# Graph-attention layers on one core: rows of scores asked for one head ahead, and stores of pieces moved to another queue

## The chip, the cores and the metric

The kernel runs on one core of a Trainium2 chip. The metric is the device time of one execution in microseconds, the median of the runs shown. One further execution was taken with the hardware profiler; the times inside the kernel are from it. Engines are called TensorE (PE), VectorE (DVE), ScalarE (ACT), GpSimd (POOL) and SyncE (SP). SyncE here only issues DMAs. A DMA can be issued from SyncE's, ScalarE's or GpSimd's queue; each queue works in order.

## What is computed

Four layers on 3327 nodes with 512 features, a dense 0/1 adjacency of 3327 x 3327. Each layer is x + L(relu(layernorm(x))). Layers 0, 1 and 2 are graph attention with 8, 4 and 8 heads, layer 3 is a mean over neighbours. Cut to what matters:

```python
def gat(h, adj, W, a1, a2):                      # layers 0 to 2, per head
    Wh = h @ W                                   # [N, 512 / heads]
    e = leaky_relu(s1[:, None] + s2[None, :], 0.2)   # s1 = Wh @ a1, s2 = Wh @ a2
    p = softmax(where(adj > 0, e, -inf), axis=-1)    # layer 1 also has self loops
    return elu(p @ Wh)
def mean_layer(h, adj):                          # layer 3
    agg = (adj > 0) @ h / max(deg, 1)
    return relu(concat(h @ Ws + bs, agg @ Wn + bn) @ Wc + bc)
```

## The kernel before

The N x N softmax is never formed. Since leaky_relu is the larger of two lines, exp(s1 + s2) and exp(0.2 (s1 + s2)) both factor into a row term and a column term, and which of the two holds for a pair of nodes is a comparison s1 > -s2. So a head is a product of 0/1 matrices (mask and comparison) with weighted features, done on TensorE, and a row factor afterwards.

**Tiles.** The 3327 nodes are 26 tiles of 128. Rows of the result go in seven *chunks* (six of four tiles, the last of two; `chunks`). The inner index goes in five *groups* of 6, 6, 6, 4 and 4 tiles (`JG`). `attention` loops over chunks, heads and groups.

**A head.** For each head of each chunk:

- the row of scores s1 of the chunk's nodes is loaded, repeated over the 128 partitions, into `s1b` (`score_rows`, L686). `s1b` has two buffers;
- the *node terms* of the head, the weighted features cut into pieces that TensorE can multiply exactly, are loaded group by group into `ab` (L718 in layer 1, ten loads a head; L724 in layers 0 and 2, five loads a head; in layer 0 some are called `abx`). `ab` has six or seven buffers;
- `matrices` compares s1 with each inner tile's s2 on ScalarE (L674) or VectorE (L671) and masks the outcome on VectorE (L678, L680) into `tht` and `gt`. In layer 1 some groups are then cast by `real` (L643) into `ts` or `tv`;
- TensorE multiplies them with `ab` into `acc` (L766, L769 in layer 1, L773 and L776 in the others), in *passes* of two row tiles over all inner tiles. VectorE reduces `acc` (L787, L791) and scales the outcome into `A`.

**Work between the passes.** After each pass `hooks.run` does one step of the work for the next layer. For a finished row tile: `finish` adds the attention's output to x (L873 to L876, stored by L877 from GpSimd), then layer norm (L347 to L354, the small steps L352 to L354 on GpSimd), relu (L359 on ScalarE), the transpose on TensorE (L138, copied out by L142), the projection (L415), the weighting (L446 to L454), and `parts`, which cuts the node terms into a tile `pt`. In layer 2's terms and the first group of layer 1's, `pieces` does it: GpSimd clears `pt` (L381), ScalarE (L393, L399) and GpSimd (L397) fill it. In the other groups of layer 1's terms ScalarE and VectorE fill two tiles `pt` (L470, L473). One step later `send` stores what `parts` put into `L.to_store` (L551), and the scores of a whole chunk (`send_s1`, L522). `pt` has two buffers there.

**Order.** A scheduler of the framework orders the instructions of each engine, by the order of the program and by when it thinks that they are ready; the order on a queue is fixed when the program is built. At a layer's end the last chunk's tiles are taken through the same steps at once, the next layer's combined weights are multiplied (`Fusion`, L183 to L208), and the next layer begins with the first chunk. A tile that is loaded or filled waits until the buffer's last use is over. For layer 0's first head the row is asked for in advance already (`early["s1"]`).

Of the kernel before, what the change touches and what calls it, by code (L numbers as in the profile page):

```python
# [52 lines left out]
def tile_gnn(ctx: ExitStack, tc: tile.TileContext, x, adj, W0, a01, W1, al, ar, W2, a2,  # L53
             Ws, bs, Wn, bn, Wc, bc, out):
    nc = tc.nc
# [9 lines left out]
    chunks = [(t, min(PER, NT - t)) for t in range(0, NT, PER)]  # L65
# [39 lines left out]
    def dims(l):  # L105


        H = heads[l]
        DA = D // H + 1
        AO = -(-(3 * DA + 1) // 8) * 8 if l != 1 else 3 * DA + 1  # L110
        return H, DA, AO, 2 * AO

    abd = []
    for l in range(3):
        H, DA, AO, HW = dims(l)
# [19 lines left out]
    def transposed(src, pool, name, bufs=2, behind=None):  # L135
        tp = ps.tile([P, KC, P], F32, name="tp", bufs=2)
        for k in range(KC):
            tr = nc.tensor.transpose(tp[:, k, :], src[:, k * P:(k + 1) * P], ident)  # L138
            if k == 0 and behind:
                after(tr, behind)  # L140
        dst = pool.tile([P, KC, P], F32, name=name, bufs=bufs)
        copied.append(nc.scalar.copy(dst, tp).ins.name)  # L142
        return dst
# [201 lines left out]
    def norm(xt, pool, behind=None):  # L345
        st = pre.tile([P, 6], F32, name="st", bufs=4)
        bn = nc.vector.bn_stats(st, xt)  # L347
        if behind:
            after(bn, behind)
        mv = pre.tile([P, 4], F32, name="mv", bufs=4)  # L350
        stats.append(nc.vector.bn_aggr(mv[:, 0:2], st).ins.name)
        nc.gpsimd.tensor_scalar(mv[:, 2:3], mv[:, 1:2], EPS, None, op0=ALU.add)  # L352
        nc.gpsimd.tensor_tensor(mv[:, 2:3], mv[:, 2:3], neghalf, ALU.pow)
        nc.gpsimd.tensor_scalar(mv[:, 3:4], mv[:, 0:1], mv[:, 2:3], -1.0, op0=ALU.mult, op1=ALU.mult)  # L354
        return mv

    def normed(xt, mv, pool, behind=None):
        h = pool.tile([P, D], F32, name="h", bufs=2)
        act = nc.scalar.activation(h, xt, AF.Relu, bias=mv[:, 3:4], scale=mv[:, 2:3])  # L359
        if behind:  # L360
            after(act, behind)
        relus.append(act.ins.name)
        return h
# [95 lines left out]
    def parts(L, t, AB, pool, first, behind=None):  # L459

        l = L.l
        g, jj = jwhere[t]
        H, DA, AO, HW = dims(l)
        H2 = H // 2
        if l == 1 and KIND[g] != "b":
            for f in range(2):
                hs = slice(f * H2, (f + 1) * H2)
                pt = pool.tile([P, H2, 2, 2, DA], F32R, name="pt", bufs=2)
                v = pt.rearrange("p h a s d -> p s a h d")
                cp = nc.scalar.copy(v[:, 0], AB[:, :, hs])  # L470
                if behind:
                    after(cp, behind)
                nc.vector.tensor_sub(v[:, 1], AB[:, :, hs], v[:, 0].bitcast(F32))  # L473
                L.to_store.append((abd[l][g][hs, :, :, jj, :].rearrange("h a p w -> p h a w"),
                                   pt.rearrange("p h a s d -> p h a (s d)").bitcast(F32)))
        else:
            pieces(L, t, AB, pool, first, behind)
        if t == JG[g][0] + JG[g][1] - 1:
            js = slice(JG[g][0], t + 1)
            nc.vector.tensor_scalar(L.ks2[:, js], L.s12[:, 1, js, :], BIG, None, op0=ALU.mult)  # L480
            nc.vector.tensor_scalar(L.ns2[:, js], L.s12[:, 1, js, :], -1.0, None, op0=ALU.mult)

    def project_last(L, t, hT, i, behind=None):

        n = pn(t)
        c, kk = where[t]
        g, jj = jwhere[t]
        pw = ps.tile([P, D], F32, name="mm")
        for k in range(KC):
            mm = nc.tensor.matmul(pw, hT[:, k, :], L.w[i][:, k, :], start=(k == 0), stop=(k == KC - 1))  # L490
            if k == 0 and behind:
                after(mm, behind)
        L.mm = mm.ins.name
        if i == 0:
            def add():
                y = pre.tile([P, D], F32, name="AB", bufs=1)
                sm = nc.vector.tensor_add(y, pw, bias)
                if behind:
                    after(sm, stats[-chunks[-1][1]])
                move(nc.sync, y1d[c][kk * P:kk * P + n, :], y, n)  # L500
            if behind:
                return add
            add()
        else:

            pt = pre.tile([P, 2, D], F32R, name="pt")
            nc.scalar.copy(pt[:, 0], pw)
            nc.vector.tensor_sub(pt[:, 1], pw, pt[:, 0].bitcast(F32))
            nc.sync.dma_start(y2d[g][:, jj], pt.bitcast(F32))

    def send_s1(L, t, pool, first):

        c, k = where[t]
        t0, nt = chunks[c]
        if k + 1 < nt:
            return
        H = heads[L.l]
        tps = ps.tile([PER * H, P], F32, name="mm" if first else "tp", bufs=2)
        nc.tensor.transpose(tps[:nt * H], L.s12[:, 0, t0:t0 + nt, :].rearrange("p t h -> p (t h)"), ident)
        s1t = pool.tile([PER * 8, P], F32, name="s1t", bufs=2)  # L520
        nc.scalar.copy(s1t[:nt * H], tps[:nt * H])
        (nc.sync if first else nc.gpsimd).dma_start(s1d[L.l][c].rearrange("h t p -> t h p"), s1t[:nt * H])  # L522

    def node_stages(L, t, get_x, pool, first=False):

        q = {}
        late = L.l == 3 and t >= NT - 4

        def behind():
            return gone[-1] if gone else None  # L530

        def statistics():
            q["mv"] = norm(q["x"], pool, relus[-2] if first and t > 1 else behind())

        def relu():

            q["h"] = normed(q["x"], q["mv"], pool, copied[-1] if t == NT - 1 and not first else behind())

        def turn():
            b = L.mm if t == NT - 1 and not first else behind()  # L540
            q["hT"] = transposed(q["h"], mp, "A", A_BUFS[2], b) if late else transposed(q["h"], pool, "hT", 2, b)

        def own():
            if late:
                left.append(lambda: project_last(L, t, q["hT"], 0, gone[-1]))
            else:
                project_last(L, t, q["hT"], 0)

        def send():
            for to, pt in L.to_store:  # L550
                nc.sync.dma_start(to, pt)  # L551
            L.to_store = []
            send_s1(L, t, pool, first)

        if first:
            stages = [lambda: (q.update(x=get_x()), statistics(), relu(), get_x(7 if t else 2)), turn,
                      lambda: parts(L, t, scaled(L, t, projected(L, t, q["hT"], first, q.get("pws")), pool, first), pool,
                                    first), send]
            if t == 0:
                stages.insert(2, lambda: q.update(pws=projected(L, t, q["hT"], first)))  # L560
            elif t == 1:
                stages[1] = lambda: (turn(), q.update(pws=projected(L, t, q["hT"], first)))
            return stages
        stages = [lambda: q.update(x=get_x()), statistics, relu, turn]
        if L.l == 3:
            return stages + [lambda: project_last(L, t, q["hT"], 1), own]
        return stages + [lambda: q.update(pw=projected(L, t, q["hT"], first)),
                         lambda: q.update(AB=scaled(L, t, q["pw"], pool, first, behind())),
                         lambda: parts(L, t, q["AB"], pool, first, behind()), send]
# [77 lines left out]
    early = {}  # L647
# [35 lines left out]
    def score_rows(l, t0, nt, h):  # L683
        s1b = rp.tile([P, WMAX], F32, name="s1b", bufs=2)
        v = s1b[:, :nt * P].rearrange("p (k i) -> p k i", k=nt)
        nc.sync.dma_start(v, s1d[l][where[t0][0]][h].partition_broadcast(P))  # L686
        return v

    def attention(L, hooks, open_next, close):

        l = L.l
        H, DA, AO, HW = dims(l)
        DK = DA - 1
        masks = mask_tiles(0, l == 1) if l else masks0
        for c, (t0, nt) in enumerate(chunks):
            last = c + 1 == len(chunks)
            A = [mp.tile([P, D], F32, name="A", bufs=A_BUFS[l]) for _ in range(nt)]
            hook = 0
            for h in range(H):
                if last and h == H - 1:  # L700
# [3 lines left out]
                    if fusion:  # L704
                        fusion.load_biases()
                        fusion.load(0, gone[-1])
                        fusion.load(1, gone[-1])
                s1v = early.pop("s1") if "s1" in early else score_rows(l, t0, nt, h)
                ab = []
                for a in range(2 if l == 1 else 1):  # L710
                    row = []
# [19 lines left out]
                for g in range(len(JG)):  # L731
                    if g in early:
                        pv, gv = early.pop(g)
                    else:

                        pt = mp.tile([P, PER * JM * P], FP8, name="tht", bufs=10 if l == 1 else 7)
# [755 lines left out]
```

## Time and profile before

| | |
|---|---|
| median of 3 runs | 3511.09 us (3506.52 to 3512.33) |
| the profiled execution | 3507.08 us, its span 3504.9 us |
| TensorE, VectorE, ScalarE, GpSimd busy | 98%, 75%, 71%, 18% of the span |
| layer 0's attention | from about 180 to 1193 us |
| layer 1's attention | to 2042 us |
| layer 2's attention | to 3158 us, then layer 3 |
| DMA engines | 228 GB/s on average, 65% of their time on SyncE's queue, 7% on GpSimd's |
| rows of scores (L686) | 140 loads, median 6.3 us from issue to landing for 256 KB |
| stores of pieces (L551) | 78, median 5.4 us from issue to landing |

How to read it: the profile's busy time of an engine leaves out waiting and issuing. A "wait" names the instruction that waited and the one that ended its wait. In a timeline a line is a run of like instructions: start, length, engine, source line, operation, what it writes and reads, how many, and in brackets the idle time before and what ended it. L12 is line 12 of the kernel. The clock is the share of full speed that TensorE was granted.

### The profile page before, as it was taken

What the parts mean: (1) busy time and instruction counts of PE and PEld (TensorE: products, weight loads), DVE (VectorE), ACT (ScalarE), POOL (GpSimd) and SP (SyncE); (2) the same over time, 40 slices, a digit from 0 to 9 for tenths busy, and PEclk for the clock granted to TensorE, in tenths of its full rate; (3) what the DMA queues carried; (4) which work ended last, traced back from release to release, by engine and by line L of the source; (5) the groups of instructions that cost most, each with busy time, mean ns of one, the idle gap of its engine ahead of it and who ended that gap; (6) DMA issues with size and microseconds to landing.
All of it is one profiled execution on the core that took longest, in us unless ns stands there. A gap on an engine that the chain in (4) does not pass through costs nothing. (4 is left out here: it accounts for less than half of the span.)

```text
span 3504.9 us, 77607 instructions
## 1 busy us (share of the span) xinstructions
PE 3425.6 (98%) x30751; PEld 3101.0 (88%) x30751; DVE 2634.1 (75%) x5227; ACT 2502.6 (71%) x4113; POOL 620.5 (18%) x858
## 2 busy tenths in 40 slices
PE   7899999999999999999999989999999999999998
PEld 6699999999999788888888879989898989886887
DVE  7788898888888799889888868867776768682221
ACT  5787888878788888888898677767666767572111
POOL 6611222112011202222323320000000001020000
PEclk9999999999999999999999999999999999999999
DMA  7699999999967787877787976655555555586331
GB/s 209 213 287 257 253 262 253 268 259 266 246 200 248 265 289 271 288 261 273 271 287 255 341 265 194 194 179 184 189 161 190 178 176 189 164 295 260 102 109 54
DMA packets 398118, 797.71 MB, mean 228 GB/s; under 512 B 112969, under 2 KB 221844, under 8 KB 397104
## 3 DMA queue, kind: packets, MB, share of 16 engines
q1 hardware_dynamic: 363890, 723.14, 64.7%
q0 software_dynamic: 28128, 62.42, 7.3%
q10 hardware_dynamic: 5726, 7.08, 0.6%
q8 instruction: 245, 4.01, 0.5%
q14 instruction: 129, 1.06, 0.1%
HBM read 663.59 MB, written 129.64 MB: 226 GB/s over the span
## 5 line engine op out<-in xcount | busy, mean ns | idle before, releaser
L674 ACT ACTIVATE gt<-s1b,ks 128x512 fp8e4<-128x512 f32 (+1 forms) x2448 | 1448.1, 677 | 373.8 <-PE acc L776 263.7
L773 PE MATMUL acc<-ab,tht 128*128 128x195 bf16 (+1 forms) x9112 | 1550.3, 248 | 5.4 <-DVE tht L678 4.6
L776 PE MATMUL acc<-ab,gt 128*128 128x195 bf16 (+1 forms) x9112 | 1549.6, 248 | 1.7 <-DVE gt L680 1.4
L776 PEld LDWEIGHTS <-gt 128*128 128x128 fp8e4 x10744 | 1051.2, 98 | 27.1 <-issue 18.6
L773 PEld LDWEIGHTS <-tht 128*128 128x128 fp8e4 x10744 | 1051.4, 98 | 22.0 <-DVE tht L678 9.3
L678 DVE TENSOR_TENSOR tht<-gt,m 128x768 uint32<-128x768 uint32 (+3 forms) x557 | 448.5, 805 | 99.6 <-ACT gt L674 98.0
L680 DVE TENSOR_TENSOR gt<-tht,m 128x768 uint32<-128x768 uint32 (+3 forms) x557 | 447.3, 803 | 9.4
L643 ACT CAST ts<-tht 128x1536 fp32r<-128x1536 fp8e4 x208 | 301.9, 1472 | 95.0 <-PE acc L766 90.0
L671 DVE TENSOR_SCALAR gt<-s1b,ns 128x512 fp8e4<-128x512 f32 (+1 forms) x446 | 223.8, 505 | 161.9 <-PE acc L776 158.4
L766 PE MATMUL acc<-ab,ts 128*128 128x258 f32 x2496 | 333.8, 290 | 5.1 <-ACT ts L643 3.4
L766 PEld LDWEIGHTS acc<-ab,ts 128*128 128x128 f32 x2496 | 313.4, 190 | 13.3 <-ACT ts L643 3.8
L674 ACT ACTIVATE tht<-s1b,ks 128x512 fp8e4<-128x512 f32 (+1 forms) x504 | 308.1, 680 | 3.9 <-DMA s1b<-s 3.2
L1028 PE MATMUL acc<-y,mf 128*128 128x512 f32 x1352 | 309.8, 391 | 0.5 <-DVE mf L1023 0.5
L876 POOL TENSOR_TENSOR xt<-xt,e 128x512 f32<-128x512 f32 x72 | 118.5, 1646 | 1055.7 <-DVE e L875 994.8
L1028 PEld LDWEIGHTS acc<-y,mf 128*128 128x128 f32 x1352 | 253.6, 188 | 56.6 <-DVE mf L1023 0.9
L776 PE MATMUL acc<-abx,gt 128*128 128x195 bf16 (+1 forms) x1632 | 284.5, 248 | 4.2 <-DVE rc L813 2.0
L773 PE MATMUL acc<-abx,tht 128*128 128x195 bf16 (+1 forms) x1632 | 284.6, 248 | 3.7 <-DMA tr<-at 2.2
L791 DVE TENSOR_REDUCE R<-acc 128x130 f32<-128x390 f32 x416 | 214.4, 554 | 88.7 <-PE acc L776 87.7
L1025 ACT CAST mf<-m 128x768 fp32r<-128x768 fp8e4 (+1 forms) x78 | 59.1, 762 | 244.0 <-PE acc L1028 232.2
L769 PE MATMUL acc<-ab,tht 128*128 128x387 bf16 x1248 | 224.0, 328 | 6.7 <-DMA ab<-ab 4.0
L766 PE MATMUL acc<-ab,tv 128*128 128x258 f32 x1664 | 217.3, 283 | 0.0
L766 PEld LDWEIGHTS acc<-ab,tv 128*128 128x128 f32 x1664 | 206.8, 189 | 0.3
(163 smaller groups left out, 3705.4 us busy)
## 6 DMA issues: line engine op xcount, KB each, us to landing
ab<-ab SPq DMA_DIRECT2D x333, 600.0 KB, 5.4
ab<-ab SPq DMA_DIRECT2D x112, 774.0 KB, 6.4
ab<-ab SPq DMA_DIRECT2D x112, 516.0 KB, 5.4
ab<-ab SPq DMA_DIRECT2D x112, 400.0 KB, 3.7
abx<-ab SPq DMA_DIRECT2D x110, 400.0 KB, 7.3
ab<-ab SPq DMA_DIRECT2D x56, 582.0 KB, 7.1
s1b<-s SPq DMA_DIRECT2D x120, 256.0 KB, 6.3
m<-mask SPq DMA_DIRECT2D x69, 384.0 KB, 4.7
```

The lines of the kernel that those rows point to most:

```text
L643: (nc.scalar.copy if KIND[g] == "s" else nc.vector.tensor_copy)(t[:, :k1 - k0, :nj], th[a][g][:, k0:k1])
L671: nc.vector.tensor_scalar(gv[:, :, jj, :], s1v, L.ns2[:, j, h:h + 1], 2.0, op0=ALU.is_gt, op1=ALU.mult, saturate=False)
L674: nc.scalar.activation(gv[:, :, jj, :], s1v, AF.Relu, bias=L.ks2[:, j, h:h + 1], scale=BIG, saturate=False)
L678: nc.vector.tensor_tensor(pu, gu, mu, ALU.bitwise_and)
L680: nc.vector.tensor_tensor(gu, pu, mu, ALU.bitwise_xor)
L766: mm = nc.tensor.matmul(acc[k][:, :2 * DA], thr[g][:, k - ks[0], jj, :], ab[a][g][:, jj, :], start=(j == 0), stop=(j == NT - 1), skip_grou ...
L769: mm = nc.tensor.matmul(acc[k][:, :3 * DA], th[a][g][:, k, jj, :], ab[a][g][:, jj, :3 * DA], start=(j == 0), stop=(j == NT - 1), skip_grou ...
L773: nc.tensor.matmul(acc[k][:, :3 * DA + o], th[0][g][:, k, jj, :], ab[0][g][:, jj, :3 * DA + o], start=(j == 0), stop=False, skip_group_che ...
L776: mm = nc.tensor.matmul(acc[k][:, AO:AO + 3 * DA + o], th[1][g][:, k, jj, :], ab[0][g][:, jj, AO:AO + 3 * DA + o], start=False, stop=(j == ...
L791: nc.vector.tensor_reduce(R[:, k], v.rearrange("p a (s d) -> p a d s", s=3), AX.X, ALU.add)
L876: nc.gpsimd.tensor_add(xt, xt, e)
L1028: nc.tensor.matmul(acc[k], mf[:, jj, :], y2[g][:, jj, s, :], start=(j0 + jj == 0 and s == 0), stop=(j0 + jj == NT - 1 and s == 1))
```

## The change

The row of scores for the next head is asked for in the program just before the present head's `ab` loads: the next head of the same chunk, or the first of the next chunk, or the first head of the next layer. Layer 2's last head asks for none. And `send` issues the stores of pieces from GpSimd's queue.

```diff
         def send():
             for to, pt in L.to_store:
-                nc.sync.dma_start(to, pt)
+                nc.gpsimd.dma_start(to, pt)
             L.to_store = []
             send_s1(L, t, pool, first)
...
                 s1v = early.pop("s1") if "s1" in early else score_rows(l, t0, nt, h)
+                if h + 1 < H:
+                    early["s1"] = score_rows(l, t0, nt, h + 1)
+                elif not last:
+                    early["s1"] = score_rows(l, *chunks[c + 1], 0)
+                elif l < 2:
+                    early["s1"] = score_rows(l + 1, *chunks[0], 0)
                 ab = []
```

The first layer's own terms are not stored by `send` but in `pieces` (L407, L408), which stays on SyncE. The prediction says first, second and third layer for layers 0, 1 and 2.

## The prediction

> **What bounds the kernel now.** I read the head of the page first, then the waits of TensorE stage by stage, the timelines of SyncE's queue and of ScalarE at the stage where TensorE waits, and the windows there.
>
> ```profile
> span 3504.9 us, 77607 instructions
> PE 3425.6 (98%) x30751; PEld 3101.0 (88%) x30751; DVE 2634.1 (75%) x5227; ACT 2502.6 (71%) x4113; POOL 620.5 (18%) x858
> ```
>
> TensorE is the bound: 3425.6 of 3504.9 us busy. All that an edit of queues can win is in the other 79.3 us, and only where a row of scores, an `ab` load or a stored piece is what TensorE waits for. Before 180 us (the first projection) neither part of the change acts, since its stores keep SyncE's queue. From 180 to 1955 us, its waits add up to 18.0 us, of which 2.4 are for an `ab` load and none for a row; after 2110 us nothing waits for scores or pieces. What is left is the turn from the second to the third layer. TensorE's waits in 1955 to 2110 us (in total, times, longest):
>
> ```profile
> PE acc L766 <- ACT ts L643: 3.4, 1, 3.4
> PE acc L773 <- DVE tht L678: 3.4, 1, 3.4
> PE acc L766 <- DMA ab<-ab: 1.7, 1, 1.7
> PE acc L769 <- DMA ab<-ab: 1.6, 1, 1.6
> ...
> PE acc L769 <- DVE tht L678: 0.6, 1, 0.6
> ```
>
> The first and the last of these are the last head of the second layer, which waits for its compares (L674) and their casts (L643). Why the compares are late stands in SyncE's queue, 2003 to 2026 us (start, length, issues), and in ScalarE's timeline:
>
> ```profile
> 2002.80 2.19 SPq L718 DMA_DIRECT2D ab<-ab  x2
> 2005.09 7.60 SPq L551 DMA_DIRECT2D ab<-pt  x2
> 2012.74 0.58 SPq L686 DMA_DIRECT2D s1b<-s  x1
> 2013.41 11.65 SPq L718 DMA_DIRECT2D ab<-ab  x8
> ...
> 2019.41 7.29 ACT L674 ACTIVATE tht<-s1b,ks 128x256 fp8e4<-128x256 f32 x18 [2.26 <-DMA s1b<-s]
> ```
>
> Both things that the change touches are in these lines: the row of scores is asked for at 2012.74, behind two stores of pieces of which the second waits 6.2 us for its copy (L399). The row's buffer had been free since 1972.3, where ScalarE's and VectorE's compares of two heads earlier end. The compares of this head start as the row lands, 2019.41. In the windows the clock shows what such a gap costs besides (columns: PE, PEld, DVE, ACT, POOL busy; clock; DMA):
>
> ```profile
> 2010.00:2015.00 5.00, 5.00 (x38) 4.10 (x37) 3.98 (x6) 2.48 (x7) 3.83 (x6) 1.00 0.70 207
> 2025.00:2030.00 5.00, 1.89 (x10) 1.89 (x11) 5.00 (x15) 4.59 (x8) 0.12 (x1) 0.85 1.03 411
> 2030.00:2035.00 5.00, 5.00 (x35) 4.78 (x35) 3.69 (x8) 4.22 (x6) 0.53 (x1) 0.81 1.02 411
> 2060.00:2065.00 5.00, 2.53 (x9) 1.89 (x10) 3.72 (x5) 5.00 (x12) 0.01 (x1) 0.76 0.18 52
> 2065.00:2070.00 5.00, 4.90 (x29) 3.92 (x28) 4.00 (x7) 3.34 (x9) 2.22 (x3) 0.90 0.27 91
> ```
>
> After each 3.4 us gap the granted clock falls: 0.15 x 5 + 0.19 x 5 = 1.7 us of work lost at the first, 0.24 x 5 + 0.10 x 5 = 1.7 us at the second.
>
> **Part 1, rows one head ahead.** No instruction is added; 140 row requests (L686) move up in program order. In most heads nothing can move in time: there are two `s1b` buffers, so the row of a head waits for the compares of two heads before in either program. The timelines show requests already there: in the first layer, chunk 3, the compares of head 2 end at 673.5 and the row of head 4 goes out at 676.5; in the second layer 1418.8 (last head of chunk 1) and 1419.1 (second head of chunk 2). The queue is not in program order, and requests were already pulled up. So this part is worth nothing, except where SyncE came late: the last head of the second layer (40 us after its buffer was free) and the first of the third (2041.69, where the buffer was free at 1985.7).
>
> Stall A, the last head of the second layer: 0.6 + 3.4 us of wait and 1.7 us of clock, 5.7 us. With the row landed by about 1980 the compares follow the freed mask tiles, and ScalarE is idle enough (2.48 of 5 us in 2010 to 2015). I take all of it.
>
> Stall B, the first head of the third layer: 3.4 + 1.7 = 5.1 us. Here an early row is not all: the compares stand behind the last tile's normalization (L359, 2057.03) in ScalarE's queue and start at 2057.75, although the row asked for at 2041.69 needs only the median 6.3 us to land. The nearest row is the turn from the first to the second layer, where the row was early (asked for at 1172.9) and the compares still began at 1207.32, right behind L359. There TensorE waits 2.1 us for L678, and the clock loses 1.7 us (0.77 and 0.89 in 1210 to 1220): 3.8 us. So B should shrink to that, by 1.3 us; its ends are 0 and 5.1.
>
> What new wait could part 1 make? A request now stands ahead of its predecessor's `ab` loads, and if the queue kept that order these loads would wait for compares. In the third layer, chunk 3, the request for head 5 would stand ahead of the loads of head 4 and wait for the compares of head 3, which end at 2613.5; these loads start at 2628.0 anyway, held by TensorE's use of the buffers. Cover: 14.5 us. In the first layer, chunk 3, it is 673.5 against 670.1 for the loads of head 3, whose matmuls begin at 695.3; a delay of 3.4 us would still leave 18 us. Nothing.
>
> **Part 2, stores from GpSimd's queue.** 78 issues (L551) leave SyncE: 52 of 512 runs each and 26 of 1024. On SyncE each took 0.37 us and the waits before them 126.5 us for copies:
>
> ```profile
> SPq L551 <- ACT pt L399: 88.3, 22, 20.2
> SPq L551 <- DVE pt L473: 38.2, 23, 9.4
> ```
>
> For those on GpSimd, the nearest rows are its own issues: 0.64 us for 128 runs (L877), 0.80 for 512 (L199), from which I estimate 1.1 us for 1024. The sum is 52 x 0.80 + 26 x 1.1 = 70 us, on an engine that is 18% busy; nothing of it is TensorE's. Landing is 4.5 us from GpSimd (L877) against 5.4 from SyncE (L551). Queued behind a store there are the additions (L876), the statistics (L352 to L354), which ScalarE's L359 and then TensorE's transposes need, the clearing of `pt` (L381), and the row stores (L877, L522). But a store's own GpSimd half (L397) stands ahead of it in this queue, and it ends with or after ScalarE's half: 2002.54 against 2001.5, 2012.29 against 2011.7. So the long waits of SyncE mostly vanish rather than move, and the rest has a whole hook step, at least 8.8 us (one pass of 104 matmuls at 84 ns), before TensorE needs it. I take 0 for that.
>
> The gain is on SyncE: the loads of 2013.41 could go at about 2005, when the stores no longer hold them. That is the other half of stall A, not a second gain. For the `ab` waits of 1.6 and 1.7 us at 1975 and 1979, SyncE gets rid of one issue of 0.39 us at 1965.46: 0.4 us.
>
> One rule speaks against the move: the Trainium skill, SBUF — State Buffer, "SBUF: two separate sides", says that GpSimd can't write descriptors while VectorE runs a mode that takes the shared port, and gives 620 ns growing to 3100 ns. The trace's 255 issues from GpSimd took 0.52 to 1.11 us beside a VectorE that is 75% busy, so it doesn't show such a stall; by the page, 78 x 2.5 = 195 us would be an estimate of the delay, still on GpSimd.
>
> **Sum.** 5.7 + 1.3 + 0.4 = 7.4 us. The profiled execution took 3507.1 us (its span and 2.2 around it), 4.0 under the median of the runs, 3511.1; against its own time 3499.7, against the median 3503.7.
>
> **Rivals.** *The gain is taken back.* The DMA engines are at 0.98 to 1.0 in most of 1960 to 2055 us, and an `ab` load then takes up to 10.5 us, against seven buffers of about 1.4 us of matmuls each (a head of ten loads in 14.5 us, 1961.6 to 1976.1). Without stall A TensorE asks for the last head's second half earlier, and waits as it did at 1975 and 1979, 3.3 us: 3511.1 - 7.4 + 3.3 = 3507. Against it: the engines fall to 0.70 at 2010 to 2015, where SyncE is held. If the row was not the limit at all, it is 3511.
>
> *Slower: GpSimd's queue becomes the wait.* A store that waits for a copy holds the statistics of the next tile, and TensorE, which works in order, stops at the transpose. This decides once a store holds GpSimd for longer than the 8.8 us of a hook step. The longest waits on SyncE are 20.2 and 9.4 us; moved whole they'd cost 11.4 + 0.6 us and the clock twice 1.7: 15.4, less 7.4 won, 3519. For it: GpSimd is busiest just there (4.6 of 5 us at 2000 to 2005), and it already waits 110.8 us in all at L381 for stores to land. Against it: L397's place in the queue.
>
> **How the numbers follow.** Two-tenths of a per cent, 7 us, is about what a measurement of this kernel can tell from no change. The forecast, with all that is better than it (B and the `ab` waits gone too: 3511.1 - 5.7 - 5.1 - 3.3 = 3497), has 0.45: faster. Taken back, or no effect: 0.27, same. GpSimd's queue, or an order of queues that I can't see: 0.28, slower. The likeliest is 3503.7, its own range 3497 to 3507; since the slower case has more than 2 in 10, the range for all goes to 3521.
>
> **What would show it.** Right: the row of the second layer's last head asked for near 1975, its compares starting before 2010, no wait for L643 and no clock under 1.0 there, and still a wait of some 2 us for L678 at the start of the third layer; L551 on GpSimd at 0.8 to 1.1 us. Wrong: waits of L138 for L359, or of L359 for L354, longer than before in the second layer's last chunk; `ab` waits growing past 3.3 us; or TensorE's waits moving to stages that I call untouched.

## The result and the profile after

Over 22 runs of each, the changed kernel took 3515.56 us in the median (3511.49 to 3521.87) and the kernel before 3507.66 us (3503.05 to 3512.34): a ratio of 1.0024, 95% interval [1.0018, 1.0029]. It is slower, by about 8 us. (The three runs of before that the prediction starts from had a median of 3511.09 us, 3.4 us above that of the 22.) The profiled execution took 3514.96 us. In after, the lines from 709 on have moved by 6: the `ab` loads are L724 and L730, the matmuls L772, L775, L779 and L782, `finish` is L879 to L883.

The head of the page of after:

```profile
span 3513.2 us, 77600 instructions
PE 3428.5 (98%) x30751; PEld 3102.4 (88%) x30751; DVE 2643.0 (75%) x5227; ACT 2502.5 (71%) x4113; POOL 691.4 (20%) x936
```

GpSimd does 78 instructions more in 70.9 us, which is the 70 us of the prediction. TensorE's work is the same; it waits more. Its waits from 1955 to 2110 us (total, times, longest):

```profile
PE tp L138 <- ACT h L359: 6.1, 1, 6.1
PE acc L772 <- DMA ab<-ab: 3.3, 2, 2.4
PE mm L415 <- ACT hT L142: 3.2, 2, 2.5
PE mm L415 <- DVE AB L454: 2.2, 1, 2.2
PE acc L779 <- DVE tht L678: 1.1, 1, 1.1
PE acc L775 <- DMA ab<-ab: 0.7, 1, 0.7
```

Stall A, the 3.4 us for L643, is gone, and of stall B's wait 1.1 us is left. In their place stand four waits for the node-term chain (L359, L142, L454), 11.5 us where before had 1.6, the largest a transpose that waits 6.1 us for a normalized tile. All waits of this stretch add up to 17.4 us, where before had 13.1. The clock adds to it; here are windows around the largest wait (columns as in the prediction):

```profile
2055.00:2060.00 5.00, 0.92 (x3) 0.09 (x1) 1.23 (x3) 1.26 (x2) 2.93 (x6) 0.94 0.17 62
2060.00:2065.00 5.00, 2.28 (x7) 1.68 (x8) 2.59 (x6) 1.87 (x3) 4.44 (x8) 0.50 0.35 108
2065.00:2070.00 5.00, 5.00 (x14) 3.86 (x13) 0.17 (x1) 4.20 (x7) 1.04 (x3) 0.53 0.43 107
```

The granted clock was one half for 10.24 us from 2059.42, which is still inside this gap (2055.92 to 2062.04), and for 3.41 us each after the gaps of 2.50 us (from 1981.59) and 2.24 us (from 2008.45): 17.07 us in the stretch, against 6.83 before. Not all of that is lost, since TensorE stands idle in a part of it: of the 10.24 us it worked 6.94. In windows over just these times it worked 13.8 us at half clock, in before 6.4, and half of such work is lost: 6.9 us against 3.2. So the turn costs 4.3 us more in waits and 3.7 us more in clock, 8.0 us. The rest of the two profiles differs by less: 1.6 us less at an `ab` wait near 1280 us, 1.7 us less of clock near 1213 (the wait before it is 2.1 us in both), and 2.3 us more in the first layer, whose end moves by as much from one profile to the next (see below). That makes 7.0 of the profiles' 8.3 us; where the other 1.3 us lie is not shown.

Why the normalized tile is late stands in GpSimd's timeline (start, length, operation, in brackets the idle time before and what ended it). After:

```profile
2006.44 1.10 POOL L551 DMA_DIRECT2D ab<-pt  x1
...
2015.40 0.17 POOL L381 MEMSET pt<- 128x80 bf16 x1 [7.29 <-DMA ab<-pt]
...
2017.17 2.11 POOL L397 TENSOR_TENSOR pt<-r 128x520 bf16<-128x520 f32 x2
2020.46 1.00 POOL L551 DMA_DIRECT2D ab<-pt  x1 [1.18 <-ACT pt L399]
2029.16 0.17 POOL L381 MEMSET pt<- 128x80 bf16 x1 [7.70 <-DMA ab<-pt]
...
2034.65 0.93 POOL L551 DMA_DIRECT2D ab<-pt  x1
2045.68 0.17 POOL L381 MEMSET pt<- 128x80 bf16 x1 [10.10 <-DMA ab<-pt]
...
2048.65 0.93 POOL L551 DMA_DIRECT2D ab<-pt  x1
2056.91 0.17 POOL L381 MEMSET pt<- 128x80 bf16 x1 [7.33 <-DMA ab<-pt]
2057.04 1.25 POOL L882 TENSOR_TENSOR A<-A,e 128x512 f32<-128x512 f32 x1
```

The same stretch before:

```profile
2009.78 2.51 POOL L397 TENSOR_TENSOR pt<-r 128x520 bf16<-128x520 f32 x2
...
2013.24 0.17 POOL L381 MEMSET pt<- 128x80 bf16 x1 [0.36 <-DMA ab<-pt]
...
2014.68 2.07 POOL L397 TENSOR_TENSOR pt<-r 128x520 bf16<-128x520 f32 x2 [0.81 <-DVE r L389]
...
2046.45 1.27 POOL L876 TENSOR_TENSOR A<-A,e 128x512 f32<-128x512 f32 x1 [1.82 <-DVE e L875]
```

`pt` has two buffers, so the tile after next is cleared (L381) only when this tile's store has landed. In after the clear stands directly behind that very store, and the third pieces (L397) of the tile *between* stand behind the clear. So GpSimd waits out a landing at every tile, and the two buffers work like one: the stores follow each other in 14.0, 14.2 and 14.0 us, where before had two of them 7.2 and 5.0 us apart. The first of the last chunk's two additions (L882, L876 before) starts at 2057.04 instead of 2046.45, and L354 on GpSimd, L359 on ScalarE and the transpose L138 follow it:

```profile
2060.88 0.26 POOL L354 TENSOR_SCALAR mv<-mv 128x1 f32<-128x1 f32 x1
2061.17 0.81 ACT L359 ACTIVATE h<-A,mv 128x512 f32<-128x512 f32 x1 [1.56 <-POOL mv L354]
```

GpSimd's waits of L381 for a landing in this stretch, after and then before:

```profile
POOL pt L381 <- DMA ab<-pt: 39.5, 5, 10.1
POOL pt L381 <- DMA ab<-pt: 6.4, 3, 3.7
```

### The profile page after: what moved, and what is told of

Same layout as the page of the kernel before. It is cut to its first block, busy times and chain, and to the rows that moved or that the text cites. A ratio compares the mean times of both kernels' runs of the same rounds, so it can differ in the third digit from the quotient of the medians.

```text
span 3513.2 us, 77600 instructions
## 1 busy us (share of the span) xinstructions
PE 3428.5 (98%) x30751; PEld 3102.4 (88%) x30751; DVE 2643.0 (75%) x5227; ACT 2502.5 (71%) x4113; POOL 691.4 (20%) x936
## 3 DMA queue, kind: packets, MB, share of 16 engines
q0 software_dynamic: 40224, 109.63, 11.2%
## 4 chain that ended last, share of the span: by engine, by line
PE 86%; ACT 3%; DVE 2%; DMA 2%; issue 1%; POOL 1%; SPq 0%; POOLq 0%; DVEq 0%; ACTq 0%
PE acc L782 24%; PE acc L779 24%; PE acc L772 12%; PE acc L1034 9%; PE acc L775 5%; PE mm L490 5%; PE mm L415 5%; DMA tr<-at 1%; ACT gt L674 1%; PE tp L138 1%; PE acc L415 1%; DVE tht L678 0%; ACT tht L674 0%; PE mm L190 0%; DVE gt L680 0%
## 5 line engine op out<-in xcount | busy, mean ns | idle before, releaser
L674 ACT ACTIVATE gt<-s1b,ks 128x512 fp8e4<-128x512 f32 (+1 forms) x2448 | 1447.9, 677 | 375.3 <-PE acc L782 266.2
L779 PE MATMUL acc<-ab,tht 128*128 128x195 bf16 (+1 forms) x9112 | 1552.8, 248 | 3.9 <-DVE tht L678 3.1
L782 PE MATMUL acc<-ab,gt 128*128 128x195 bf16 (+1 forms) x9112 | 1551.8, 248 | 2.6 <-DVE gt L680 2.3
L782 PEld LDWEIGHTS <-gt 128*128 128x128 fp8e4 x10744 | 1052.7, 98 | 28.6 <-issue 18.3
L779 PEld LDWEIGHTS <-tht 128*128 128x128 fp8e4 x10744 | 1052.5, 98 | 21.7 <-DVE tht L678 8.9
L643 ACT CAST ts<-tht 128x1536 fp32r<-128x1536 fp8e4 x208 | 301.8, 1471 | 82.9 <-PE acc L772 76.6
L772 PE MATMUL acc<-ab,ts 128*128 128x258 f32 x2496 | 332.3, 289 | 0.0
L772 PEld LDWEIGHTS acc<-ab,ts 128*128 128x128 f32 x2496 | 311.9, 189 | 8.0 <-issue 0.7
L674 ACT ACTIVATE tht<-s1b,ks 128x512 fp8e4<-128x512 f32 (+1 forms) x504 | 308.6, 680 | 0.7
L882 POOL TENSOR_TENSOR xt<-xt,e 128x512 f32<-128x512 f32 x72 | 116.1, 1613 | 958.5 <-DVE e L881 876.7
L782 PE MATMUL acc<-abx,gt 128*128 128x195 bf16 (+1 forms) x1632 | 284.0, 248 | 4.8 <-DVE gt L680 2.8
L779 PE MATMUL acc<-abx,tht 128*128 128x195 bf16 (+1 forms) x1632 | 284.1, 248 | 4.3 <-DVE tht L678 4.3
L775 PE MATMUL acc<-ab,tht 128*128 128x387 bf16 x1248 | 223.8, 327 | 3.7 <-DVE tht L678 2.1
L772 PE MATMUL acc<-ab,tv 128*128 128x258 f32 x1664 | 220.2, 284 | 3.9 <-DMA ab<-ab 3.3
L772 PEld LDWEIGHTS acc<-ab,tv 128*128 128x128 f32 x1664 | 208.5, 190 | 5.2 <-issue 3.9
```

The lines of the kernel that those rows point to most:

```text
L643: (nc.scalar.copy if KIND[g] == "s" else nc.vector.tensor_copy)(t[:, :k1 - k0, :nj], th[a][g][:, k0:k1])
L674: nc.scalar.activation(gv[:, :, jj, :], s1v, AF.Relu, bias=L.ks2[:, j, h:h + 1], scale=BIG, saturate=False)
L772: mm = nc.tensor.matmul(acc[k][:, :2 * DA], thr[g][:, k - ks[0], jj, :], ab[a][g][:, jj, :], start=(j == 0), stop=(j == NT - 1), skip_grou ...
L775: mm = nc.tensor.matmul(acc[k][:, :3 * DA], th[a][g][:, k, jj, :], ab[a][g][:, jj, :3 * DA], start=(j == 0), stop=(j == NT - 1), skip_grou ...
L779: nc.tensor.matmul(acc[k][:, :3 * DA + o], th[0][g][:, k, jj, :], ab[0][g][:, jj, :3 * DA + o], start=(j == 0), stop=False, skip_group_che ...
L782: mm = nc.tensor.matmul(acc[k][:, AO:AO + 3 * DA + o], th[1][g][:, k, jj, :], ab[0][g][:, jj, AO:AO + 3 * DA + o], start=False, stop=(j == ...
```

## The experiments

Theory T: it is this clear behind its store, in the third layer's terms. Rival R1: the early rows upset the queues. Rival R2: the issues and their traffic themselves. Each kernel ran in 11 or 12 timed runs beside the kernel before. The table has, besides, three numbers of each profile: the time from the first matmul of the second layer to the first of the third, TensorE's waits from 1955 to 2110 us, and the time at half clock there. This last one counts idle time at half clock too, and it scatters: runs 1 and 12 are the same kernel and have 6.8 and 10.2 us.

| kernel | ratio to before [95%] | 2nd to 3rd layer, us | waits, us | half clock, us |
|---|---|---|---|---|
| before | 1 | 849.8 | 13.1 | 6.8 |
| after | 1.0024 [1.0018, 1.0029] | 857.6 | 17.4 | 17.1 |
| 1 rows alone | 0.9997 [0.9988, 1.0006] | 847.4 | 12.3 | 6.8 |
| 2 stores alone | 1.0025 [1.0016, 1.0034] | 860.2 | 18.0 | 17.1 |
| 3 after, third layer's stores on SyncE | 0.9997 [0.9988, 1.0006] | 848.3 | 13.3 | 6.8 |
| 4 after, second layer's stores on SyncE | 1.0022 [1.0013, 1.0031] | 862.4 | 20.2 | 17.1 |
| 5 after, cleared once | 0.9992 [0.9983, 1.0001] | 844.6 | 11.3 | 3.4 |
| 6 as 4, cleared once | 0.9997 [0.9988, 1.0006] | 850.2 | 12.5 | 6.8 |
| 7 after, clear behind the third pieces | 1.0005 [0.9996, 1.0014] | 844.3 | 10.0 | 3.4 |
| 8 as 1, compares on ScalarE | 0.9991 [0.9982, 1.0000] | 846.2 | 12.0 | 3.4 |
| 9 as 1, compares held | 0.9983 [0.9974, 0.9992] | 847.9 | 10.9 | 10.2 |
| 10 as 7, compares held | 0.9993 [0.9984, 1.0002] | 848.7 | 10.1 | 3.4 |
| 11 as 5, compares held | 0.9994 [0.9986, 1.0003] | 845.3 | 10.0 | 3.4 |
| 12 rows alone, again | 0.9996 [0.9987, 1.0004] | 847.7 | 12.5 | 10.2 |
| 13 as 9, again | 0.9994 [0.9984, 1.0003] | 847.8 | 12.3 | 6.8 |
| 14 one row early | 1.0002 [0.9994, 1.0011] | 847.0 | 12.1 | 10.2 |

The three with the third layer's stores on GpSimd and the clear as the scheduler puts it (after, 2, 4) stand apart in every column.

**The two parts apart.** Run 1 is after with `send` back on SyncE:

```diff
-                nc.gpsimd.dma_start(to, pt)
+                nc.sync.dma_start(to, pt)
```

> Part 1 without part 2. Theory T (the clear of pt, L381, stands right behind a store on GpSimd and waits until that store has landed, 7 to 10 us, with the additions and statistics of the last chunk queued behind it): without stores on GpSimd the loss is gone and stall A's gain stays: about 7 us under before, 3501 us; waits of L381 for a landing 10 to 12 us in 1955 to 2130 us as in before, not 39.5, and no wait of TensorE for L643. Rival R1 (the rows asked for early upset the order of the queues, the stores are innocent): as after, 8 us above before. Rival R2 (the 78 issues and their traffic themselves, not the wait behind them): 3501 us too.

Run 2 is before with `send` on GpSimd's queue.

> Part 2 without part 1. T: the order on GpSimd is that of after (store, clear, statistics), so its loss stays, 13 to 15 us at the last turn, and stall A goes only in part, since its row is no longer behind two stores: 8 to 15 us above before, with a wait of L138 for L359 of some 6 us. R1: the time of before, within 2 us. R2: as T.

Measured: the rows alone 3505.13 us against 3508.84, in the ratio of the runs 1 us faster, -4 to +2; the stores alone 3516.06, 9 us slower. The loss belongs to the stores, and R1 falls. Run 2 has the wait of L138 for L359, and 38.3 us of L381 waiting:

```profile
PE tp L138 <- ACT h L359: 8.2, 1, 8.2
```

But the 7 us under before that T left to the rows alone did not come either; that is the second question below.

**Which stores.**

```diff
-                nc.gpsimd.dma_start(to, pt)
+                (nc.gpsimd if L.l == 1 else nc.sync).dma_start(to, pt)     # run 3; run 4: L.l == 2
```

> After, but only the second layer's terms are stored from GpSimd; the third layer's 26 stores stay on SyncE. T: the loss is at the turn to the third layer, where only the third layer's stores run, so it goes: 3501 to 3504 us. R1: as after. R2: between after and the rows alone, by the share of the issues' time (26 of 78 stores, 26 x 0.93 = 24 of 70 us): some 3 us under after.

> After, but the second layer's 52 stores go back to SyncE; only the third layer's 26 leave from GpSimd. It is the complement of the run with the third layer's on SyncE. T: the whole loss at the last turn stays: waits of L381 for a landing about 40 us in 1955 to 2130 us, a wait of L138 for L359 of 6 to 8 us, 6 to 9 us above before. Rival F (the 52 stores of the second layer, issued while the first layer's attention keeps the DMA engines busy, cost the first layer some 3 us): the first layer ends at about 1193 us as in before, not 1195 to 1197. If the loss lay in the second layer's stores, the time of before.

With only the second layer's 52 stores on GpSimd the time is that of the rows alone (3508.75 us; the 3501 to 3504 of T counted on part 1's gain); with only the third layer's 26 the loss is whole (3515.93 against 3507.10 us). Run 4's waits, TensorE's and then GpSimd's:

```profile
PE tp L138 <- ACT h L359: 7.4, 1, 7.4
PE mm L415 <- ACT hT L142: 5.1, 3, 2.9
```

```profile
POOL pt L381 <- DMA ab<-pt: 39.1, 5, 9.4
```

So a third of the issues carries all of the loss, which speaks against R2. Rival F of the second text is not borne out: the first layer ended at 1191.5 us in run 4, but at 1196.9 and 1195.8 us in runs 8 and 12, which have all stores on SyncE as well. Run 12 is the kernel of run 1, where the layer ended at 1192.4. So these 3 to 5 us differ from one profile to the next, whatever the queue.

**The clear.** Run 5 keeps two tiles `pt` for the third layer's terms and sets their constant columns once; 24 of 26 clears are left out.

```diff
-        if o == 0:
+        if o == 0 and not (l == 2 and t > 1):
             L.pt = pool.tile(...)
+        if l == 2:
+            if t < 2:
+                both.append(L.pt)
+            L.pt = both[t % 2]
         pt = L.pt
-        nc.gpsimd.memset(...)
+        if l != 2 or t < 2:
+            nc.gpsimd.memset(...)
```

> After, but the third layer's terms use two tiles pt whose constant columns are set once, so that no clear stands behind a store (24 of its 26 clears are left out; the result stays). T: GpSimd waits for no landing ahead of the additions, the wait of L138 for L359 and the half clock of 10 us go: 12 to 15 us under after, about 6 under before, 3501. R1 and R2: as after, within 3 us, since neither the rows nor the issues change.

Run 7 leaves everything in and only tells the scheduler that a clear may not go ahead of L397 of the tile before; no wait is added on the chip.

```diff
+        if l == 2 and thirds:                # ones: the clear of this tile
+            after(ones, thirds[-1])
...
+        thirds.append(th.ins.name)      # th: the last L397 of this tile
```

> After with every instruction kept: in the third layer's terms a clear (L383 here) may not be placed ahead of the third pieces (L401 here) of the tile before it, so that it stands one tile later on GpSimd and waits for a store that has had a hook step to land. T, in its narrower form (it is the place of the clear, ahead of the pieces of the tile between, that makes every tile of the last chunk cost a landing): the stores of the last chunk are again under 10 us apart in places, not 14 us each, the wait of L138 for L359 goes below 2 us, and the time is within 3 us of the run with the clear set once, 8 to 12 us under after. If any wait for a landing on GpSimd costs as much, wherever it stands: as after, 6 to 9 us above before.

Both take the loss away: 0.9992 and 1.0005, each interval wholly under that of after. By their ratios they are 11 and 7 us under after, a little less than the 12 to 15 and 8 to 12 that were expected, and 4.6 us apart where 3 was the limit; their intervals overlap. GpSimd's timeline in run 7 (L383 is the clear, L401 the third pieces, L556 the store, L887 the addition):

```profile
2004.20 1.11 POOL L556 DMA_DIRECT2D ab<-pt  x1
...
2012.49 2.56 POOL L401 TENSOR_TENSOR pt<-r 128x520 bf16<-128x520 f32 x2 [1.64 <-DVE r L393]
2014.99 0.17 POOL L383 MEMSET pt<- 128x80 bf16 x1
2015.35 1.05 POOL L556 DMA_DIRECT2D ab<-pt  x1 [0.19 <-issue]
...
2027.75 0.93 POOL L556 DMA_DIRECT2D ab<-pt  x1
...
2034.88 0.93 POOL L556 DMA_DIRECT2D ab<-pt  x1
2037.57 0.17 POOL L383 MEMSET pt<- 128x80 bf16 x1 [1.76 <-DMA ab<-pt]
2045.16 1.27 POOL L887 TENSOR_TENSOR A<-A,e 128x512 f32<-128x512 f32 x1 [7.42 <-DVE e L886]
```

The store of 2004.20 landed at 2012.93, as slowly as in after, but the clear that needs it comes 2 us later and waits for nothing. The stores follow each other in 11.2, 12.4 and 7.1 us, and the addition now waits for VectorE, not for a landing. That settles T in its narrow form: the issues are all still there and the landing is as long; what decides is the place of one 0.17 us instruction behind it.

Run 6 has run 4's stores and run 5's tiles.

> The run before this one in the list, with the constant columns of the third layer's two tiles pt set once (24 clears left out, the result stays). T: no wait of GpSimd for a landing ahead of the additions, so 3 to 6 us under before. With F as well: the first layer ends near 1193 us and it is the fastest so far, about 2 us under the run with the clear set once and all stores on GpSimd. Without F: equal to that run.

It took 3506.17 us against 3507.10: the 9 us of run 4 are gone again, though it is 1 us under before and not the 3 to 6 of the text. The first layer ended at 1194.7 us, so F gains nothing here either.

**Where the gain of part 1 went.** In the rows alone TensorE's waits of the stretch still add up to 12.3 us. The timeline of ScalarE in run 1 shows compares (L674) standing ahead of the weighting (L446, L449) and the copies, and TensorE now waits for VectorE; first the timeline, then the waits:

```profile
1999.13 2.91 ACT L674 ACTIVATE tht<-s1b,ks 128x256 fp8e4<-128x256 f32 x7
2001.95 0.20 ACT L446 ACTIVATE AB<-s 128x8 f32<-128x8 f32 x1
```

```profile
PE acc L779 <- DVE tht L678: 3.1, 1, 3.1
PE mm L415 <- DVE AB L454: 2.4, 2, 1.9
PE acc L775 <- DMA ab<-ab: 2.4, 2, 1.9
PE tp L519 <- DVE s L435: 2.2, 1, 2.2
```

The waits for L454 and L435 before:

```profile
PE mm L415 <- DVE AB L454: 0.7, 2, 0.5
PE tp L519 <- DVE s L435: 0.3, 1, 0.3
```

Theory V: the early compares displace the node-term steps. Run 8 sends the eight compares of VectorE in the second layer's last head to ScalarE; run 9 holds that head's compares (`after(cmp, gone[-4])`, an order for the scheduler alone); runs 10 and 11 do the same on top of runs 7 and 5.

> Rows alone (stores on SyncE), and the eight compares that VectorE does for the second layer's last head go to ScalarE. Theory V (part 1 wins stall A and gives it back because the early compares and masks fill VectorE's queue from 2001 to 2026 us ahead of L454 and L435, for which TensorE then waits 1.9 and 2.2 us): these two waits shrink by 2 to 4 us together, and the time is 2 to 4 us under the rows alone. Rival (the gain is taken by the ab loads): waits for L454 and L435 as before, and the time that of the rows alone. If ScalarE can't take them in time, a wait for L643 comes back.

> Rows alone (stores on SyncE), with every instruction kept: the compares of the second layer's last head may not be placed ahead of the matmuls four half passes earlier, so that on ScalarE they stand behind the additions' L882, the normalization L359 and the weighting L446 and L449, as in before, not ahead of them. V (the early compares displace the node-term steps on ScalarE and VectorE, for which TensorE then waits at L454 and L435): the wait for L454 goes from 1.9 back to 0.7 or less, that for L435 from 2.2 to under 0.5, the wait for L643 stays away; 3 to 5 us under the rows alone, 4 to 6 under before. If the compares are too late now: a wait for L643 of 1 to 3 us and the time of the rows alone.

> After with the clear behind the third pieces of the tile before, and with the compares of the last head held as in the run before this one; nothing is left out. T and V together: no wait of L138 for L359, none for L643, those for L454 and L435 under 1 us; 4 to 7 us under before. If only T holds: as the clear behind the third pieces alone, within 2 us of it.

> The clear set once (24 clears left out, the result stays), all stores on GpSimd, rows early, and the compares held. T and V: as the run before this one within 2 us, 4 to 8 us under before, the fastest of all. If only T holds: as the clear set once alone.

Run 8: the wait for L435 fell to 1.0 us, that for L454 stayed at 2.4, and a new one of 1.1 us for L880 on ScalarE came; its ratio is 2 us under that of the rows alone, with intervals that overlap widely. Run 9 was the fastest by its ratio, but its profile had 2.0 us at L435 and 1.4 at L454 as well as the 3.4 us of stall B. In runs 10 and 11 the wait for L454 was 0.5 us, against 2.8 in runs 7 and 5, and that for L435 was absent, as it was in runs 7 and 5 already; a wait of 1.2 us for a compare came instead. Their times are about 2 us under before, not the 4 to 8 expected, and no time moved beyond the intervals. So runs 1 and 9 ran again, on one chip, with a kernel that is before with a single row asked for early, the one of stall A:

```diff
                 s1v = early.pop("s1") if "s1" in early else score_rows(l, t0, nt, h)
+                if l == 1 and last and h == H - 2:
+                    early["s1"] = score_rows(l, t0, nt, h + 1)
```

> Rows alone once more, beside the next two on one chip. If part 1 is worth about 1 us (its waits moved, not removed): 3 us under before to 2 above. If it is worth the 7 us of the prediction: 5 to 8 under.

> Rows alone with the last head's compares held, once more. If its 6 us under before came from the held compares: again 3 to 9 under before, and 2 us or more under the rows alone. If not (its profile still had the waits of 2.0 us for L435 and 1.2 us for L454, and took 847.9 us from the first matmul of the second layer to the first of the third, the rows alone 847.4): the time of the rows alone, within 3 us.

> Before, with one row asked for early: that of the second layer's last head; the 139 others as in before. If the others are worth nothing, as the prediction has it: the time of the rows alone within 3 us, no wait for L643 of over 1 us at the last head, and stall B of 5 us as in before. If the other rows cost something: faster than the rows alone by 3 us or more.

The rows alone gave 0.9996, the held compares 0.9994, the one row 1.0002. The 6 us of run 9 did not come back: run 13 is 2.7 us under run 12 in the medians and 0.7 in the ratios, within the intervals. Holding the compares is not shown to be worth anything. The one row does what all 140 do; its waits:

```profile
PE tp L519 <- DVE s L435: 3.3, 1, 3.3
PE acc L775 <- DVE tht L678: 3.1, 1, 3.1
PE mm L415 <- DVE AB L454: 2.1, 2, 1.9
```

So no row elsewhere shows a cost or a gain, within the 3 us that the intervals leave, and the one row's gain of 3.4 + 0.6 us is met by 4.4 us more at L435 and L454 (5.4 us, before 1.0) in the same stretch. The wait for L435 has its own 3.41 us at half clock (from 2026.39), as stall A had (from 2028.47). That the gain is given back to these two waits is shown by the kernel with nothing else in it. That it is the place of the compares that delays L454 and L435 is only argued from the timelines: the runs that moved the compares moved the waits about and not the time.

No version beats before beyond doubt. Run 9 is the best candidate, 0.9983 and then 0.9994, the second interval reaching 1.0003. Runs 5, 7, 10 and 11 all beat after.

## Why the prediction was wrong

**Part 2, the cover.** The step that failed is "the rest has a whole hook step, at least 8.8 us", from which followed "I take 0 for that". The prediction names what is queued behind a store, the clearing of `pt` among it, and costs only how long the store itself waits for its copies. It did not ask what the clear waits for. The clear waits for that store's landing, and once both are in one queue the order decides: 7.3 to 10.1 us at each of four tiles. The 8.8 us was also the wrong stage's step. The loss is in the second layer's last chunk, where a head takes 14.5 us in two passes and `attention` calls `hooks.run` twice in each, so 3.6 us a step. The term of 0 was 8 to 9 us (runs 2 and 4). In the turn, the waits of these two add up to 4.9 and 7.1 us more than before, and the clock takes 1.8 and 2.1 us more (10.1 and 10.7 us of work at half clock, before 6.4).

**Part 2, the landing.** "Landing is 4.5 us from GpSimd (L877)" was the wrong row: the median of the 78 stores was 7.7 us from GpSimd, and the four of the last chunk took 8.2 to 11.0. After and before:

```profile
DMA to landing us min/median/max: 3.4/7.7/11.6
DMA to landing us min/median/max: 3.2/5.4/10.5
```

The second row rests on the 20 stores whose landing the trace of before shows. In the last chunk SyncE's stores landed no faster, where it shows: 8.5 us in before, 8.4 and 9.2 in run 3. How much of the long landing is the queue's and how much the stretch's is not shown. L877 stores 128 runs of 2 KB; these stores consist of 512 or 1024 runs of 776 to 1032 bytes. The issues took 0.75 to 1.52 us, 69.5 us in all: that term held.

**Part 1.** Stall A's own wait went as forecast: the row was asked for at 1989.23, the compares started at 1999.74, no wait for L643.

```profile
1989.23 0.42 SPq L686 DMA_DIRECT2D s1b<-s  x1
1999.74 0.49 ACT L674 ACTIVATE tht<-s1b,ks 128x256 fp8e4<-128x256 f32 x1
```

The row went out 14 us later than the "near 1975" of the prediction, which did no harm. But "no clock under 1.0 there" did not hold: in after it was one half for 3.41 us from 2011.63, behind a wait for L454. "I take all of it" failed: run 14 shows 4.4 us of new waits for VectorE in the same stretch. ScalarE's idle time was looked at (2.48 of 5 us busy); VectorE, 3.98 of 5 us busy in the same row of the windows, was not. Of stall B the rows alone keep 3.1 of 3.4 us; in after, and in runs 2 and 4, it is 1.1 us, behind a wait of 6.1 to 8.2 us of L138. Nor is the 1.7 us of clock that was taken over from the first turn a fixed price: in after the same wait of 2.1 us there brought no half clock. The `ab` waits did not shrink by 0.4 us: 3.4 us in the rows alone, 4.0 in after, before 3.3.

**The rivals.** The slower rival had the side and the place: GpSimd's queue, the statistics behind a store, the transpose, and both signs of "wrong" (L138 waiting for L359, `ab` waits over 3.3 us) came. Its mechanism was not the one that acted. Stores did wait long for copies on GpSimd, 191.5 us for L473 against 38.2 on SyncE, so the waits did move and grow: the 40 stores of L470 and L473 have no GpSimd half, so the prediction's argument of L397's place in the queue does not reach them. But these are the second layer's stores, and run 3, which keeps all of them there, lost nothing. Its evidence "it already waits 110.8 us in all at L381 for stores to land" was the clue to the real one. That its sum, 8 us over before, is what was measured is luck: its store waits cost nothing, and the 7.4 us that it subtracts were never won. The rival in which the gain is taken back describes the rows alone (0.9997), but through `ab` loads, whose waits stayed at 3.4 us; VectorE's results took it.

## What to carry to other kernels

Before a store moves to a queue of an engine that also computes, look for an instruction on that engine that reuses the stored buffer: if it stands directly behind the store, it waits out the landing (here 7.3 to 10.1 us) with everything behind it, and double buffering is lost when the scheduler puts it ahead of the other buffer's work. A wait that is taken away can come back at another busy engine, as it did here; read the busy columns of every engine that the freed work lands on, not only of the one that was late. Price a gap of TensorE with its clock, and count only the work that falls into the half clock.

## What the runs showed of the hardware

The granted clock changed between 1.0 and 0.5, and its times at 0.5 inside the layers are whole multiples of 3.41 us. The changes of after lie on one grid of 3.41 us: 1984.33, 2011.63 and 2059.42 are 8 and 14 steps apart. A gap of 2.24 us brought one such step (3.41 us of work at half clock, 1.7 us lost), the gap of 6.12 us three (10.24 us, 6.94 of them work, 3.5 us lost). Whether a gap brings one at all varies: 1.90 us (run 1, from 2002.42) did; 2.35 us (after, from 2040.69) and 3.07 us (run 3, from 2060.24) did not. The Trainium skill, TensorE: Matmul & The Clock Gate, "What's actually happening", tells of the same two states and of a free-running window of 3413 ns, which the rows bear out. Its table gives at least one idle window of about 3.4 us as the condition; here gaps of 1.9 to 2.5 us sufficed several times.
